# Which PSUM evictions the counting products wait for, in a convolution-attention and mixture-of-experts kernel

## The chip, the cores and the metric

The kernel runs on one core of one Trainium2 chip. The metric is the device time of one execution in microseconds; the time of the kernel before is the median of three runs.

## The reference, cut to what matters

Eight images of 256 channels by 32 x 32 positions pass two layers. Layer 0 projects each image to queries, keys and values (8 heads of 64), takes the softmax of the scores over the queries, and projects back. Layer 1 is an attention over the 1024 tokens of an image and then a mixture of 8 experts, of which each token uses its best two:

```python
logits = tokens.astype(jnp.float32) @ router_w.astype(jnp.float32).T
probs = jax.nn.softmax(logits, axis=-1)
rw, re = jax.lax.top_k(probs, TOP_K)
...
combine = jnp.zeros((N, E), tokens.dtype).at[jnp.arange(N)[:, None], re].set(rw)
...
for e in range(E):
    h = jax.nn.gelu(tokens @ w1[e] + b1[e], approximate=False)
    y = h @ w2[e] + b2[e]
    out = out + combine[:, e:e + 1] * y
```

Everything is float32.

## The kernel before, in words

The images go through the core one after the other (b = 0 to 7). For images 0 to 6 the tokens are sorted by expert and the experts run once over all seven images (`experts`); image 7 runs all experts over all its tokens (`dense`). To sort, the kernel needs for every token how many earlier tokens chose the same expert. It gets that from two small matrix products in `dispatch` (L820), here called the counting products: a strictly triangular matrix `before` (L832) and a matrix of ones (L833), each times `both`, the 128 x 64 table that marks the two experts of each token. Each writes 64 columns of PSUM. `d_cn` (L835) is VectorE's copy of the 128 columns into SBUF; the row addresses and the scatters to DRAM follow from it later.

`dispatch` is a generator. The routing of image b is advanced in steps by `share()` (L567) inside `layer0` of image b + 1, so the counting products run seven times, in layer 0 of images 1 to 7.

`layer0` (L441) walks 32 steps: four head pairs g, and for each eight blocks j of 128 keys. In a step, for two heads h, TensorE computes scores into a PSUM tile of two banks (`score`, L461, L468); VectorE takes the maximum of each bank (`first_max`, L483, and `second_max`, L492); ScalarE takes the exponential of both banks (`soften`, L509); VectorE divides (`divide`, L523, L525); and two steps later TensorE multiplies by the values (`gather_values`, L533, L545). The score tiles come from `ps_big`, a pool of three buffers of two banks each, in rotation.

At fixed steps (`PROJECT`, L454; step j = 3 for g = 0) the queries and keys of the next head pair are made by `project_pair` (L341). It takes one tile `pq` of that same pool and fills it twice, the queries first and then the keys. Each time, two products of 512 columns go to bank 0 and two to bank 1 (L350); each bank is then read out by ScalarE with the bias (`evict`, L315). So there are four evictions: queries bank 0, queries bank 1, keys bank 0, keys bank 1. They are called first to fourth below. The dependencies are kept by a tracker that sees one tile where there are two banks; where two accesses lie in different banks, the code takes the dependency away by hand (`declare_no_dep`, L359).

For g = 0 the counting products come directly after the eight products of `project_pair` (L621 to L623): `share(pq)` sends the tile to `dispatch`, and both counting products write columns 0 to 127 of it, which lie in bank 0. The next instructions of TensorE are held behind them by `issue_after(counted.ins)` (L579 to L588): the scores of the next step, `score(at, 0, 0)` and `score(at - 1, 1, 1)`, and then `gather_values(at - 2, 0)`. On VectorE, the copy to `d_cn` stands directly ahead of the second maximum of the interrupted step. On ScalarE the fourth eviction is followed by the exponential of that step.

Of the kernel before, what the change touches and what calls it, by code (L numbers as in the profile page):

```python
# [19 lines left out]
def kernel(  # L20
# [23 lines left out]
    nc = tc.nc  # L44
    P = 128
    B, C, S = x.shape
    E, D, FF = w1.shape
# [4 lines left out]
    NT = S // P  # L52
# [22 lines left out]
    def big(name):  # L75

        return ps_big.tile([P, 1024], F32, tag="big", name=name)
# [78 lines left out]
    ones = const.tile([P, P], F32, name="ones")  # L156
    nc.gpsimd.memset(ones, 1.0)

    before = const.tile([P, P], F32, name="before")
# [151 lines left out]
    def evict(dst, pq, g, t, scalar):  # L311

        scale = SCALE if t == 0 else 1.0
        if scalar:
            return nc.scalar.activation(  # L315
                dst, pq, AF.Identity, bias=b_qks[:, t, g : g + 1], scale=scale
            )
        return nc.vector.tensor_scalar(
            dst, pq, b_qk[:, t, g : g + 1], scale, ALU.add, ALU.mult
        )  # L320
# [20 lines left out]
    def project_pair(b, xT, g):  # L341


        pq = big(f"pqk_{b}_{g}")
        dsts, left = [], []
        for t in range(2):
            dst = two.tile([P, S], F32, tag=f"qk{t}", name=f"qk{t}_{b}_{g}")
            for n in range(NH2):
                for cc in range(NCC):
                    mm = nc.tensor.matmul(  # L350
                        pq[:, ts(n, 512)],
                        wqkv[:, cc, t, ts(g, P)],
                        xT[:, cc, ts(n, 512)],
                        start=(cc == 0),
                        stop=(cc == NCC - 1),
                    )
                    for at, ins in left:
                        if at != n:
                            tc.declare_no_dep(mm.ins, ins, reason="the other bank")  # L359
                left.append((n, evict(dst[:, ts(n, 512)], pq[:, ts(n, 512)], g, t, True).ins))  # L360
            dsts.append(dst)
        return dsts, pq, mm

    class Begin:

# [75 lines left out]
    def layer0(b, xT, begun, routing, xs):  # L441
# [132 lines left out]
        for at in range(last + LAG + 1):  # L574
# [38 lines left out]
            if at <= last and (g, j) in PROJECT:  # L613
                with tc.issue_after(firsts[at, 1].ins), tc.issue_after(array.ins):
                    share(firsts[at, 1])
                    pair, pq, mm = project_pair(b, xT, g + 1)
                qks.append(pair)
                if (g, j) == PROJECT[-1]:
                    with tc.issue_after(firsts[at, 1].ins):
                        t1 = residual(b, xs)  # L620
                if g == 0:  # L621
                    with tc.issue_after(mm.ins), tc.issue_after(firsts[at, 1].ins):
                        counted = share(pq)  # L623
                if b == B - 1 and (g, j) == PROJECT[-1]:
                    with tc.issue_after(firsts[at, 1].ins):
                        plan(groups[0])
            elif at <= last and (g, j) > PROJECT[1]:
                share(firsts[at, 1])
# [191 lines left out]
    def dispatch(b, n2, l, group):  # L820

        gate, hots = yield from gates(b, l)

        def tmp(tag):
            return small.tile([P, NT, E], F32, tag=tag, name=f"{tag}_{b}", bufs=1)


        both = tmp("d_both")
        nc.vector.tensor_add(both, hots[0], hots[1])
        pcn = yield  # L830
        flat = both.rearrange("p i e -> p (i e)")
        nc.tensor.matmul(pcn[:, : NT * E], before, flat, start=True, stop=True)  # L832
        counted = nc.tensor.matmul(pcn[:, NT * E : 2 * NT * E], ones, flat, start=True, stop=True)  # L833
        cn = small.tile([P, 2, NT, E], F32, tag="d_cn", name=f"d_cn_{b}", bufs=1)
        nc.vector.tensor_copy(cn.rearrange("p t i e -> p (t i e)"), pcn[:, : 2 * NT * E])  # L835
        yield counted
        per = small.tile([P, E, NT], F32, tag="d_per", name=f"d_per_{b}", bufs=1)
        nc.vector.tensor_copy(per, cn[:, 1].rearrange("p i e -> p e i"))
        upto = small.tile([P, E, NT], F32, tag="d_upto", name=f"d_upto_{b}", bufs=1)
        nc.vector.tensor_tensor_scan(  # L840
            upto.rearrange("p e i -> p (e i)"),
            later.rearrange("p e i -> p (e i)"),
            per.rearrange("p e i -> p (e i)"),
            0.0,
            ALU.mult,
            ALU.add,
        )
        rows = tmp("d_rows")
        nc.vector.tensor_sub(rows.rearrange("p i e -> p e i"), upto, per)
        nc.vector.tensor_add(rows, rows, cn[:, 0])  # L850
        counts = keep.tile([P, E], F32, tag="counts", name=f"counts_{b}")
        if group.counts is None:
            nc.vector.tensor_copy(counts, upto[:, :, NT - 1])
        else:
            nc.vector.tensor_add(
                rows, rows, group.counts.unsqueeze(1).to_broadcast([P, NT, E])
            )
            nc.vector.tensor_add(counts, group.counts, upto[:, :, NT - 1])
        group.counts = counts

        kept = []
        ats = []
        for k in range(2):
            hot = hots[k]
            sel = tmp("d_sel")
            nc.vector.tensor_mul(sel, hot, rows)
            row = keep.tile([P, NT], F32, tag=f"row{k}", name=f"row{k}_{b}")
            nc.vector.tensor_reduce(row, sel, AX.X, ALU.add)
            nc.vector.tensor_mul(sel, hot, e_iota.unsqueeze(1).to_broadcast([P, NT, E]))
            exp = keep.tile([P, NT], F32, tag=f"exp{k}", name=f"exp{k}_{b}")  # L870
            nc.vector.tensor_reduce(exp, sel, AX.X, ALU.add)
            to = small.tile([P, NT], F32, tag="d_to", name=f"d_to_{b}_{k}", bufs=2)
            nc.vector.scalar_tensor_tensor(to, exp, float(group.cap), row, ALU.mult, ALU.add)
            kept.append((row, exp))
            at = small.tile([P, NT], I32, tag=f"d_at{k}", name=f"d_at{k}_{b}", bufs=1)
            nc.vector.tensor_copy(at, to)
            ats.append(at)
        group.kept[b] = gate, kept

        for k in range(2):  # L880
            for i in range(NT):
                behind = yield
                view = group.views[2 * (NT * group.items.index(b) + i) + k]
                scatter = nc.gpsimd.indirect_dma_start(  # L884
                    out=view[:, :],
                    out_offset=bass.IndirectOffsetOnAxis(ap=ats[k][:, i : i + 1], axis=0),
                    in_=n2[:, i, :],
                    in_offset=None,
                )
                if behind is not None:  # L890
                    tc.add_manual_dep(scatter.ins, behind.ins.name, BEHIND)
# [420 lines left out]
    for b in range(B):  # L1312
        xT = next_x
        if b + 1 < B:
            next_x = load_x(b + 1)
        if b > 0:
            xs = load_squares(b)
        t1 = layer0(b, xT, begun, routing, xs)
        if b + 1 < B:
            begun = Begin(b + 1, next_x)  # L1320
            t2 = attend(b, t1, begun.at)
            n2, _, l = normed(b, t2, begun.at)
            nc.sync.dma_start(groups[0].sums[b], t2)
            routing = dispatch(b, n2, l, groups[0])
            continue
        experts(groups[0])
        others = Results(groups[0])
        others.begin()
        norm = None

        def fill(place):

            nonlocal norm
            others.tick(place)
            if place == "last products":
                norm = Norm(t1, one.tile([P, NT, D], F32, tag="xa", name=f"n2_{b}"), 1e-5, f"f{b}")
                return norm.blocks(0, NT - 1)

        t2 = attend(b, t1, fill, others.tick)
        dense(b, t2, norm, others.tick)  # L1340
        assert others.added == len(others.units) and not others.whole
# [42 lines left out]
```

## Time and profile before

| what | value |
| --- | --- |
| median of three runs (lowest, highest) | 2407.27 us (2404.34, 2408.37) |
| the profiled execution | 2406.31 us |
| its span in the profile | 2404.6 us, granted TensorE clock 0.994 |
| projections of a pair, L350 | 384 records, mean 599 ns |
| evictions, L315 | 124, mean 691 ns |
| counting products, L832 and L833 | 14 records each, mean 297 and 275 ns |
| copy to `d_cn`, L835 | 7, mean 291 ns |
| scores L468, gathered values L545 | 4096 records each, mean 594 and 592 ns |

The profile has one row per instruction, with a start and a duration, on separate tracks for TensorE's products (PE) and its weight loads (PEld), VectorE (DVE), ScalarE (ACT), GpSimd (POOL) and the DMA queue of SP. A float32 product appears as two records, each with its own weight load: 192 products on L350 make 384 records. A row of a timeline begins with start and duration, and may merge several records (x3 at its end); the duration then covers all of them. What stands in square brackets is the idle time of that track just before the row, and what ended it.

### The profile page before, as it was taken

How to read it: one execution, taken by the hardware profiler on the slowest of the kernel's cores; microseconds unless marked ns; L12 is line 12 of the kernel's file. 1: busy time of each engine (PE TensorE's matmuls, PEld its weight loads, DVE VectorE, ACT ScalarE, POOL GpSimd, SP SyncE). 2: the span in 40 equal slices, each digit the busy share in tenths (PEclk: the TensorE clock that was granted, in tenths of full speed). 3: DMA queues.
4: the chain of work that ended last, by engine and by line, in shares of the span. 5: the costliest groups of instructions: out<-in, count | busy, mean ns of one | idle time of the engine just before them, and what ended most of it. 6: DMA issues, size and time to landing. Idle time of an engine off the chain costs nothing.

```text
span 2404.6 us, 36813 instructions
## 1 busy us (share of the span) xinstructions
PE 2359.7 (98%) x13759; PEld 1316.5 (55%) x13759; DVE 1540.9 (64%) x3660; ACT 938.0 (39%) x1570; POOL 420.0 (17%) x391
## 2 busy tenths in 40 slices
PE   9999999999999999999999999999999999999898
PEld 3356534654466336633664356435653388887565
DVE  5775587457845785578647864687468753334776
ACT  3651366126611662156315641465136622221111
POOL 0000012000200020003000200020002234444563
PEclk9999999999999999999999999999999999999899
DMA  8993201010101010001000100100010256665454
GB/s 294 386 386 101 53 19 36 1 36 12 43 1 35 8 47 1 18 18 54 1 18 18 47 8 6 31 25 12 1 36 19 74 176 220 219 219 161 142 170 119
DMA packets 114778, 196.59 MB, mean 82 GB/s; under 512 B 15752, under 2 KB 58408, under 8 KB 112808
## 3 DMA queue, kind: packets, MB, share of 16 engines
q1 hardware_dynamic: 88504, 126.52, 15.8%
q0 software_dynamic: 25008, 67.20, 9.1%
q8 instruction: 109, 1.79, 0.3%
q10 hardware_dynamic: 1088, 0.52, 0.1%
q14 instruction: 69, 0.57, 0.1%
HBM read 108.88 MB, written 110.90 MB: 91 GB/s over the span
## 4 chain that ended last, share of the span: by engine, by line
PE 91%; DVE 5%; ACT 2%; DMA 1%; issue 1%; POOL 0%; SPq 0%; DVEq 0%; ACTq 0%; POOLq 0%
PE po L545 19%; PE psc L468 18%; PE py L695 9%; PE ps L670 7%; PE pqk L350 7%; PE pr L636 5%; PE ph L1021 4%; PE pv L387 4%; PE pe L1046 4%; PE pdh L1250 2%; PE px L655 2%; PE pdy L1274 2%; PE pa L689 2%; PE pqk L328 2%; PE px L1011 1%
## 5 line engine op out<-in xcount | busy, mean ns | idle before, releaser
L509 ACT ACTIVATE ex<-psc,nmax 128x1024 f32<-128x1024 f32 x512 | 570.5, 1115 | 312.6 <-DVE scrap L492 227.8
L468 PE MATMUL psc<-qk,qk 64*64 64x512 f32 x4096 | 578.4, 594 | 10.3 <-ACT ex L509 10.3
L545 PE MATMUL po<-ex,vs 64*64 64x512 f32 x4096 | 573.5, 592 | 1.3 <-DVE vs L525 0.3
L492 DVE TENSOR_SCALAR_CACHE_REDUCE scrap<-psc,nmax 128x512 f32<-128x512 f32 x512 | 384.4, 751 | 152.0 <-PE psc L468 126.2
L483 DVE TENSOR_REDUCE nmax<-psc 128x1 f32<-128x512 f32 x512 | 350.3, 684 | 9.3 <-PE psc L468 9.3
L468 PEld LDWEIGHTS psc<-qk,qk 64*64 64x64 f32 x4096 | 181.0, 132 | 285.8 <-ACT ex L509 138.0
L545 PEld LDWEIGHTS po<-ex,vs 64*64 64x64 f32 x4096 | 177.9, 132 | 273.5 <-issue 81.7
L695 PE MATMUL py<-n,aT 128*128 128x256 f32 x1024 | 238.0, 386 | 2.9 <-DVE aT L691 2.9
L670 PE MATMUL ps<-nT,xa 128*128 128x512 f32 x512 | 236.0, 592 | 0.0
L695 PEld LDWEIGHTS py<-n,aT 128*128 128x128 f32 x1024 | 191.7, 191 | 66.6 <-DVE aT L691 41.8
L884 POOL DMA_INDIRECT rows<-n,d_at x112 | 108.8, 972 | 662.6 <-DVE nmax L483 662.3
L681 ACT ACTIVATE ex<-ps,nmax 128x1024 f32<-128x1024 f32 x64 | 71.3, 1115 | 348.0 <-DVE nmax L678 333.5
L815 POOL TENSOR_TENSOR t<-t,n 128x2048 f32<-128x2048 f32 x8 | 36.3, 4534 | 924.0 <-DVE n L242 924.0
L350 PE MATMUL pqk<-xT,wqkv 128*128 128x512 f32 x384 | 171.2, 599 | 0.0
L701 DVE SCALAR_TENSOR_TENSOR t<-py,rs,t 128x256 f32<-128x256 f32 x64 | 30.9, 482 | 194.4 <-PE py L695 194.4
L670 PEld LDWEIGHTS ps<-nT,xa 128*128 128x128 f32 x512 | 93.5, 190 | 81.2 <-issue 75.1
L350 PEld LDWEIGHTS pqk<-xT,wqkv 128*128 128x128 f32 x384 | 71.0, 190 | 99.9 <-issue 77.8
L1130 POOL DMA_INDIRECT yk<-y,yat x112 | 110.6, 988 | 72.4 <-issue 26.8
L636 PEld LDWEIGHTS pr<-wo,res 128*128 128x128 f32 x512 | 120.7, 331 | 3.7 <-ACT res L563 3.7
L636 PE MATMUL pr<-wo,res 128*128 128x256 f32 x512 | 121.6, 398 | 0.3 <-ACT res L563 0.3
L387 PE MATMUL pv<-wqkv,xT 128*128 128x512 f32 x256 | 120.3, 599 | 1.4 <-DVE v L395 1.0
L315 ACT ACTIVATE qk<-pqk,b_qks 128x512 f32<-128x512 f32 x124 | 85.6, 691 | 88.9 <-PE pqk L350 79.8
(189 smaller groups left out, 2479.8 us busy)
## 6 DMA issues: line engine op xcount, KB each, us to landing
rows<-wb SPq DMA_DIRECT2D x7, 8192.0 KB, 51.7
y<-yb SPq DMA_DIRECT2D x63, 256.0 KB, 2.4
xs<-in_x_dram SPq DMA_DIRECT2D x64, 128.0 KB, 3.9
out_dram<-oT SPq DMA_DIRECT2D x60, 128.0 KB, 2.9
xT<-in_x_dram SPq DMA_DIRECT2D x7, 1024.0 KB, 5.0
sums<-t SPq DMA_DIRECT2D x7, 1024.0 KB, 3.9
o<-sums SPq DMA_DIRECT2D x7, 1024.0 KB
wpack<-in_L_ffn_w_dram SPq DMA_DIRECT2D x4, 1024.0 KB
```

What stands on the lines that cost most here:

```text
L350: mm = nc.tensor.matmul(pq[:, ts(n, 512)], wqkv[:, cc, t, ts(g, P)], xT[:, cc, ts(n, 512)], start=(cc == 0), stop=(cc == NCC - 1),)
L387: nc.tensor.matmul(pv, self.xT[:, cc, ts(i, P)], wqkv[:, cc, 2, :], start=(cc == 0), stop=(cc == NCC - 1),)
L468: mm = nc.tensor.matmul(pss[at, h][ts(c, DK), ts(n, 512)], k[r, j * P + c * DK : j * P + (c + 1) * DK], q[r, ts(n, 512)], start=True, stop ...
L483: firsts[at, h] = nc.vector.tensor_reduce(nmax, pss[at, h][:, ts(0, 512)], AX.X, ALU.max, negate=True)
L492: seconds[h] = nc.vector.tensor_scalar(scrap, pss[at, h][:, ts(1, 512)], -1.0, nmaxes[at, h], ALU.mult, ALU.min, accum_out=nmax,)
L509: nc.scalar.activation(ex, pss.pop((at, h)), AF.Exp, bias=nmaxes.pop((at, h)), scale=1.0, accum_out=sums[at][:, h : h + 1],)
L545: mm = nc.tensor.matmul(po[n][ts(h, DK), :], vss[at][keys, h, :], exps[at, h][keys, ts(n, 512)], start=(j == 0 and turn == 0), stop=(j == ...
L636: nc.tensor.matmul(pr[:, :C], own(res[:, g, :], i), wo[:, g, :], start=(g == 0), stop=(g == NPAIR - 1))
L670: nc.tensor.matmul(psc[:, ts(n, 512)], xa[:, ec, ts(i, P)], nT[:, ec, ts(n, 512)], start=(ec == 0), stop=(ec == NCC - 1),)
L695: nc.tensor.matmul(py[:, :D], aT[:, ts(m, P)], n1[:, m, :], start=(m == 0), stop=(m == NT - 1))
L884: scatter = nc.gpsimd.indirect_dma_start(out=view[:, :], out_offset=bass.IndirectOffsetOnAxis(ap=ats[k][:, i : i + 1], axis=0), in_=n2[:, ...
L1130: ins = nc.gpsimd.indirect_dma_start(out=self.slot(at)[:, k, :], out_offset=None, in_=self.group.y[:, :], in_offset=bass.IndirectOffsetOnAxis(
```

## The change

`project_pair` returns, with the tile, the list of those of its evictions that read bank 1. `dispatch` makes the same two counting products in a loop, and takes the dependency on those evictions away from each. The matrices, the columns and the order are as they were.

```diff
@@ project_pair @@
-        return dsts, pq, mm
+        return dsts, (pq, [ins for n, ins in left if n > 0]), mm
@@ dispatch @@
-        pcn = yield
+        pcn, others = yield
         flat = both.rearrange("p i e -> p (i e)")
-        nc.tensor.matmul(pcn[:, : NT * E], before, flat, start=True, stop=True)
-        counted = nc.tensor.matmul(pcn[:, NT * E : 2 * NT * E], ones, flat, start=True, stop=True)
+        for at, what in enumerate((before, ones)):
+            counted = nc.tensor.matmul(
+                pcn[:, ts(at, NT * E)], what, flat, start=True, stop=True
+            )
+            for ins in others:
+                tc.declare_no_dep(counted.ins, ins, reason="the other bank")
         cn = small.tile([P, 2, NT, E], F32, tag="d_cn", name=f"d_cn_{b}", bufs=1)
         nc.vector.tensor_copy(cn.rearrange("p t i e -> p (t i e)"), pcn[:, : 2 * NT * E])
         yield counted
```

In the built programs every engine has the same instructions in the same order before and after. Seven waits differ, one for each pair of counting products: the first of the pair waits for a count of ScalarE that is lower by one, so for the third eviction and no longer for the fourth. The copy to `d_cn` waits for the second counting product and for the fourth eviction in both programs.

## The prediction

> **What bounds the kernel now.** I read the page first: busy time by engine, then the chain that ended last.
>
> ```profile
> PE 2359.7 (98%) x13759; PEld 1316.5 (55%) x13759; DVE 1540.9 (64%) x3660; ACT 938.0 (39%) x1570; POOL 420.0 (17%) x391
> ...
> PE 91%; DVE 5%; ACT 2%; DMA 1%; issue 1%; POOL 0%; SPq 0%; DVEq 0%; ACTq 0%; POOLq 0%
> ```
>
> TensorE is the bound, so a hole in its stream that nothing else refills is lost time. The list of waits says whether the counting products make one (total us, times, longest):
>
> ```profile
> PEld pqk L832 <- ACT qk L315: 9.6, 6, 1.6
> ...
> PE pqk L832 <- ACT qk L315: 4.7, 6, 0.8
> ```
>
> Six of seven times TensorE waits for an eviction; the seventh, in image 1, is the same hole (0.83 us) under the name "issue". The timeline of the last one (start, duration, engine):
>
> ```profile
> 1792.86 0.69 ACT L315 ACTIVATE qk<-pqk,b_qks 128x512 f32<-128x512 f32 x1 [1.03 <-PE pqk L350]
> 1793.09 1.45 PE L350 MATMUL pqk<-xT,wqkv 128*128 128x512 f32 x3
> 1793.52 0.19 PEld L350 LDWEIGHTS pqk<-xT,wqkv 128*128 128x128 f32 x1 [0.24 <-issue]
> 1794.58 0.69 ACT L315 ACTIVATE qk<-pqk,b_qks 128x512 f32<-128x512 f32 x1 [1.03 <-PE pqk L350]
> 1795.31 0.30 PEld L832 LDWEIGHTS pqk<-d_both,before 128*128 128x128 f32 x2 [1.60 <-ACT qk L315]
> 1795.32 0.43 PE L832 MATMUL pqk<-d_both,before 128*128 128x64 f32 x2 [0.78 <-ACT qk L315]
> 1795.53 0.30 PEld L833 LDWEIGHTS pqk<-d_both,ones 128*128 128x128 f32 x2
> ...
> 1795.90 0.21 PEld L468 LDWEIGHTS psc<-qk,qk 64*64 64x64 f32 x8
> ...
> 1796.08 0.29 DVE L835 COPY d_cn<-pqk 128x128 f32<-128x128 f32 x1 [3.92 <-PE pqk L833]
> ...
> 1797.06 0.75 DVE L492 TENSOR_SCALAR_CACHE_REDUCE scrap<-psc,nmax 128x512 f32<-128x512 f32 x1 [0.69 <-PE psc L468]
> ```
>
> The first row is the third eviction, over at 1793.55; the fourth runs from 1794.58 to 1795.27, and the counting products start 0.04 us after it. I measure from the last weight load of the projection (1793.52, "t"): counting load t+1.79, scores t+2.38, copy t+2.56, maximum t+3.54. The other six agree within 0.03 us. In image 7, pair 1, the same projection stands without counting products:
>
> ```profile
> 1822.78 0.19 PEld L350 LDWEIGHTS pqk<-xT,wqkv 128*128 128x128 f32 x1 [0.24 <-issue]
> 1823.73 0.21 PEld L468 LDWEIGHTS psc<-qk,qk 64*64 64x64 f32 x8 [0.76 <-issue]
> ...
> 1824.64 1.04 PE L545 MATMUL po<-ex,vs 64*64 64x512 f32 x8
> ...
> 1824.89 0.75 DVE L492 TENSOR_SCALAR_CACHE_REDUCE scrap<-psc,nmax 128x512 f32<-128x512 f32 x1 [3.39 <-PE psc L468]
> ```
>
> Here the scores load at t+0.95, and the maximum starts at t+2.11, with no wait for the evictions. Seventeen such transitions (three in image 0, two in each other image) read 0.94 to 0.95.
>
> [...] the third eviction reads bank 0 while L350 writes bank 1, and takes 0.69 us like the fourth, beside which nothing is written. So I charge the new overlap nothing. [...] (loads of L350 are 0.43 us apart, beside running products)[...]. [...] so I count from starts, and not from the bracketed 0.78.
>
> **The change, part by part.** Nothing is added or moved: same instructions, same order on all queues, SP's and POOL's included. What goes is one count in the wait of seven instructions.
>
> When can the first counting product go? Its three conditions: the third eviction, over at t+0.03 and, with 0.04 to 0.07 us to be seen, at t+0.10; the table `both`, done at t-1.35 in six cases and t-3.68 in the first; the queue, whose next slot is one spacing after t, t+0.43. The queue is last. The load of `before` is 128 x 128 like L350's, so I let it be pulled ahead: t+0.43. The product behind it starts when the last L350 record has streamed, t+0.86, and the second load with it. The loads then follow at their present pace (four from 1795.31 to about 1795.64, 0.11 apart; scores 0.26 after the fourth): t+0.86, t+0.97, t+1.08, scores t+1.34. Against t+2.38 to t+2.41 that is 1.05 us. A second way: the plain transition, 0.95, plus four records of 0.11, is t+1.39, a gain of 1.00. I take 1.05; 7 x 1.05 = 7.35 us.
>
> Bounds of one gain: if the counting load isn't pulled ahead, it starts where the scores do in the plain transition, t+0.95, and the scores at t+0.95+0.59 = t+1.54: 0.85. The bracketed gap gives 0.78. If all follows at the next slot, 1.79 - 0.43 = 1.36, the largest gain possible[...]. Seven times: 5.5 to 9.5 us.
>
> What is late next? VectorE: the copy still waits for the fourth eviction, which doesn't move (t+1.06 to t+1.75). It starts at about t+1.81 and ends at t+2.10. The second maximum queued behind it needs its score, t+3.54 - 1.05 = t+2.49: 0.39 us of slack. If that cover were gone, the copy's 0.29 us would be exposed. ScalarE: the exponential now starts 0.86 us after the maximum does; it moves to about t+3.3, and ScalarE is free from t+1.75. PSUM: the score tile that takes over `pq`'s buffer starts over a microsecond after the scores restart, past the copy's new end. TensorE then runs steps of 3.43 us without a hole, as after every transition now.
>
> The sum: profiled execution 2406.31 (span 2404.6 and 1.7 around it) less 7.35 is 2399.0. It lay 1.0 under the median of 2407.27, so I forecast 2407.27 - 7.35 = 2399.9.
>
> **The rivals.**
> *Load not pulled ahead.* The plain transition speaks for it (loads wait there), the equal tile size against it. 7 x 0.85 = 6.0: 2401.3.
> *The copy stays the pace.* The copy has two waits; if VectorE starts it only where it does now, t+2.56, the maximum comes at t+2.86 and not at t+2.49. The gain is 3.54 - 2.86 = 0.68; seven make 4.8: 2402.5. For it: the copy does wait for the fourth eviction. Against: that ends 0.8 us before t+2.56.
> *Given back.* The layer norm behind layer 0, or the DMA-fed expert stage, could be tied to something that doesn't move: 2407. Against: all transfers of a stage are issued behind its own instructions, and the chain is 91% TensorE.
> *Slower: the score ring falls out of step.* VectorE has only 0.32 us idle in a step of 3.43 (two gaps, 0.19 and 0.13). If TensorE restarts earlier than VectorE by more than it regains, score tiles come free late and TensorE waits for the exponential in each of the four steps left of the pair. The waits list has weight loads waiting for that 216 times, 138.0 us, so 0.64 each: 7 x 4 x 0.64 = 17.9 us lost, 7.35 won: 2417.8. It decides from the point where the copy ends more than 0.32 us after t+2.49. Against: the plain transitions restart at t+0.95, earlier than any forecast here, and keep 3.43 us.
>
> That the edit does nothing is excluded: the seven waits differ in the built program.
>
> **How the numbers follow.** Chances: forecast 0.63, load not pulled ahead 0.15, copy 0.12, given back 0.07, slower 0.03. A measurement of this kernel tells about 0.2% (4.8 us, below 2402.5) from no change. Faster: 0.63 + 0.15 + half of the copy's 0.12 = 0.84; within: 0.06 + 0.07 = 0.13; slower 0.03. The bounds give 2407.27 - 9.5 = 2397.8 and - 5.5 = 2401.8, and 2402.5 with the copy; a median of three runs that spread over 4 us may be off by about one: 2396.8 to 2403.2. Left out are given back and slower, 0.10, and about as much for the spread.
>
> **What would show it.** Right: the wait of L832's product for the eviction is gone; its load starts at t+0.43, the scores' at t+1.34, the copy at t+1.8, the maximum at t+2.5, and seven such gains make up the span's loss. The load at t+0.95 shows the first rival; a maximum later than its score, the second; weight loads of L468 waiting longer for L509, the last. I am wrong if the scores come over 1.0 us earlier and the span doesn't.

## The result and the profile after

The changed kernel takes 2397.39 us (median of six runs, 2396.64 to 2400.2) against 2407.69 us for the kernel before in the same measurement. The ratio is 0.996, with a 95% interval of 0.9947 to 0.9973. It is faster, by 0.4%. The forecast was 2399.9; the measured time lies 2.5 us below it, inside the stated range and near its lower end. A second measurement of the same kernel, on another occasion, is among the experiments (e8_again): 2398.23 against 2406.58.

The page after the change, busy time and chain:

```profile
PE 2353.9 (98%) x13759; PEld 1313.9 (55%) x13759; DVE 1541.2 (64%) x3660; ACT 938.0 (39%) x1570; POOL 420.4 (18%) x391
...
PE 90%; DVE 5%; DMA 2%; ACT 1%; issue 1%; POOL 0%; SPq 0%; DVEq 0%; ACTq 0%; POOLq 0%
```

The totals hardly move, and would not have shown where the gain comes from. The list of waits does (total us, times, longest):

```profile
DVE d_cn L839 <- ACT qk L315: 24.2, 7, 5.4
...
PEld pqk L833 <- issue: 3.4, 14, 0.2
```

The rows in which the counting products wait for an eviction are gone. The first two weight loads of each pair follow the stream, with 0.2 us of idle track ahead of them. The wait for the eviction has moved to VectorE's copy. The last of the seven places in the timeline (start, duration, engine; line numbers behind L832 are four higher than before, and both counting products are now on L833):

```profile
1787.24 0.19 PEld L350 LDWEIGHTS pqk<-xT,wqkv 128*128 128x128 f32 x1 [0.24 <-issue]
1787.67 0.19 PEld L833 LDWEIGHTS pqk<-d_both,before 128*128 128x128 f32 x1 [0.24 <-issue]
...
1788.10 0.19 PEld L833 LDWEIGHTS pqk<-d_both,before 128*128 128x128 f32 x1 [0.24 <-issue]
1788.21 0.30 PEld L833 LDWEIGHTS pqk<-d_both,ones 128*128 128x128 f32 x2
...
1788.30 0.69 ACT L315 ACTIVATE qk<-pqk,b_qks 128x512 f32<-128x512 f32 x1 [1.03 <-PE pqk L350]
1788.58 0.21 PEld L468 LDWEIGHTS psc<-qk,qk 64*64 64x64 f32 x8
...
1789.02 0.29 DVE L839 COPY d_cn<-pqk 128x128 f32<-128x128 f32 x1 [3.13 <-ACT qk L315]
...
1789.74 0.75 DVE L492 TENSOR_SCALAR_CACHE_REDUCE scrap<-psc,nmax 128x512 f32<-128x512 f32 x1 [0.43 <-PE psc L468]
```

With t = 1787.24, the last weight load of the projection, the row of the fourth eviction (1788.30) now stands behind the counting loads and beside their products. The scores load at t+1.34 in place of t+2.38.

To take the whole effect of the seven places out of a trace, I subtract the start of the last weight load of L350 ahead of the first counting products (298.81 before, 298.79 after) from that of the last one of image 7 (1857.47 and 1850.15). This stretch holds all seven places and no stage behind layer 0 of image 7. It was 1558.66 us before and is 1551.36 after: 7.30 us shorter, 1.04 a place. Nothing else in it differs: with the two traces laid on each other weight load by weight load, the lead of the changed kernel grows by 1.04 to 1.06 us within 5 us of each place, and until the next place it moves by 0.02 us at most. The rest, from that last load to the end of the span, was 547.1 before and is 545.2 after.

### The profile page after: what moved, and what is told of

Its sections match the earlier page's. It is cut to its first block, busy times and chain, and to the rows that moved or that the text cites. A ratio compares the mean times of both kernels' runs of the same rounds, so it can differ in the third digit from the quotient of the medians.

```text
span 2395.3 us, 36813 instructions
## 1 busy us (share of the span) xinstructions
PE 2353.9 (98%) x13759; PEld 1313.9 (55%) x13759; DVE 1541.2 (64%) x3660; ACT 938.0 (39%) x1570; POOL 420.4 (18%) x391
## 4 chain that ended last, share of the span: by engine, by line
PE 90%; DVE 5%; DMA 2%; ACT 1%; issue 1%; POOL 0%; SPq 0%; DVEq 0%; ACTq 0%; POOLq 0%
PE po L545 19%; PE psc L468 18%; PE py L695 8%; PE ps L670 7%; PE pqk L350 7%; PE pr L636 5%; PE pv L387 4%; PE ph L1025 4%; PE pe L1050 4%; PE pdh L1254 2%; PE px L655 2%; PE pdy L1278 2%; PE pa L689 2%; PE pqk L328 2%; PE px L1015 1%
## 5 line engine op out<-in xcount | busy, mean ns | idle before, releaser
L509 ACT ACTIVATE ex<-psc,nmax 128x1024 f32<-128x1024 f32 x512 | 570.5, 1115 | 304.1 <-DVE scrap L492 220.4
L468 PE MATMUL psc<-qk,qk 64*64 64x512 f32 x4096 | 577.4, 593 | 10.3 <-ACT ex L509 10.3
L545 PE MATMUL po<-ex,vs 64*64 64x512 f32 x4096 | 573.2, 592 | 1.3 <-DVE vs L525 0.3
L468 PEld LDWEIGHTS psc<-qk,qk 64*64 64x64 f32 x4096 | 180.7, 132 | 285.9 <-ACT ex L509 138.3
L545 PEld LDWEIGHTS po<-ex,vs 64*64 64x64 f32 x4096 | 177.6, 132 | 273.0 <-issue 81.2
L695 PE MATMUL py<-n,aT 128*128 128x256 f32 x1024 | 236.3, 384 | 2.9 <-DVE aT L691 2.9
L695 PEld LDWEIGHTS py<-n,aT 128*128 128x128 f32 x1024 | 190.5, 190 | 66.1 <-DVE aT L691 41.8
L350 PE MATMUL pqk<-xT,wqkv 128*128 128x512 f32 x384 | 171.2, 599 | 0.0
L350 PEld LDWEIGHTS pqk<-xT,wqkv 128*128 128x128 f32 x384 | 71.0, 190 | 99.9 <-issue 77.8
```

The lines of the kernel that those rows point to most:

```text
L350: mm = nc.tensor.matmul(pq[:, ts(n, 512)], wqkv[:, cc, t, ts(g, P)], xT[:, cc, ts(n, 512)], start=(cc == 0), stop=(cc == NCC - 1),)
L468: mm = nc.tensor.matmul(pss[at, h][ts(c, DK), ts(n, 512)], k[r, j * P + c * DK : j * P + (c + 1) * DK], q[r, ts(n, 512)], start=True, stop ...
L509: nc.scalar.activation(ex, pss.pop((at, h)), AF.Exp, bias=nmaxes.pop((at, h)), scale=1.0, accum_out=sums[at][:, h : h + 1],)
L545: mm = nc.tensor.matmul(po[n][ts(h, DK), :], vss[at][keys, h, :], exps[at, h][keys, ts(n, 512)], start=(j == 0 and turn == 0), stop=(j == ...
L695: nc.tensor.matmul(py[:, :D], aT[:, ts(m, P)], n1[:, m, :], start=(m == 0), stop=(m == NT - 1))
```

## The experiments

All times after t are read as above. "The stretch" and "the rest" are those just defined, taken from each kernel's profile:

| kernel | scores load | stretch | rest | median (runs) | before beside it |
| --- | --- | --- | --- | --- | --- |
| before | t+2.38 to 2.41 | 1558.66 | 547.1 | | |
| after | t+1.34 | 1551.36 | 545.2 | 2397.39 (6) | 2407.69 |
| e1_bank1 | t+2.38 to 2.41 | 1558.71 | 548.4 | 2406.31 (12) | 2406.41 |
| e2_three | three 1.34, four 2.38 | 1555.55 | 549.9 | 2403.18 (12) | 2406.41 |
| e3_copy_free | t+1.34 | 1551.33 | 545.7 | 2399.74 (7) | 2406.41 |
| e4_four_copies | t+1.34 | 1554.22 | 548.8 | 2402.81 (12) | 2406.41 |
| e5_before_twice | t+3.10 to 3.12 | 1563.55 | 552.8 | 2411.56 (9) | 2406.58 |
| e6_after_twice | t+1.34 | 1551.15 | 549.4 | 2398.97 (6) | 2406.58 |
| e7_bf16 | t+1.01 | 1548.98 | 547.3 | 2396.83 (5) | 2406.58 |
| e8_again | t+1.34 | 1551.29 | 548.8 | 2398.23 (7) | 2406.58 |

The stretch repeats within 0.1 us for the same behaviour (after, e3, e8). The rest scatters over 7.6 us whatever the kernel, so the stretch is the sharper gauge of this change. The first four experiments ran on one chip, e5 to e8 on another, each with the kernel before beside them.

**e1_bank1: the same number of dependencies taken away, but the wrong ones.** The counting products go to columns 512 to 639 of the tile, and lose their dependency on the evictions of bank 0.

```diff
-        return dsts, (pq, [ins for n, ins in left if n > 0]), mm
+        return dsts, (pq, [ins for n, ins in left if n == 0]), mm
...
-                pcn[:, ts(at, NT * E)], what, flat, start=True, stop=True
+                pcn[:, 512 + at * NT * E : 512 + (at + 1) * NT * E], what, flat, start=True, stop=True
...
-        nc.vector.tensor_copy(cn.rearrange("p t i e -> p (t i e)"), pcn[:, : 2 * NT * E])
+        nc.vector.tensor_copy(cn.rearrange("p t i e -> p (t i e)"), pcn[:, 512 : 512 + 2 * NT * E])
```

> The counting products write bank 1 of the same tile and wait only for evictions that read bank 1; as many dependencies are taken away as in the change. Times after t, the start of the last weight load of the projection. Theory (what counts is which eviction ends the wait): the products wait for the fourth eviction again, counting load at t+1.8, scores at t+2.4, layer 0 of image 7 reaches its last projection load at 1857.5 us as before, time within 0.2% of before (2407.7). Rival (it is the smaller number of dependencies, or the loop form of the code, that gains): counting load at t+0.43 and a time as after, 2397.

Measured: ratio to before 0.9998 (0.999 to 1.0007), stretch 1558.71. The last place in its timeline:

```profile
1793.39 0.19 PEld L350 LDWEIGHTS pqk<-xT,wqkv 128*128 128x128 f32 x1 [0.24 <-issue]
1794.45 0.69 ACT L315 ACTIVATE qk<-pqk,b_qks 128x512 f32<-128x512 f32 x1 [1.03 <-PE pqk L350]
1795.19 0.30 PEld L833 LDWEIGHTS pqk<-d_both,before 128*128 128x128 f32 x2 [1.61 <-ACT qk L315]
```

The load waits for the end of the fourth eviction, as in the kernel before. So neither the loop form nor the smaller number of dependencies gains anything; what counts is which eviction is the last one waited for.

**e2_three: the change at three places of seven.**

```diff
         pcn, others = yield
+        others = others if b < 3 else []
```

> The change for the counting products of images 0 to 2 only, three places of seven. Theory (each place gives 1.05 us, independently): three transitions with scores at t+1.34 and four at t+2.39; the last projection load of image 7 at 1857.5 - 3.2 = 1854.3 us, time before less 3.2 us, 2404.5, give or take what the tail behind layer 0 does by itself. Rival (the whole measured gain of 10.3 us belongs to the places, 1.47 each): the last projection load at 1853.1, time before less 4.4, 2403.3. Rival (steps behind a place slow down again): last load near 1857.

Measured: three transitions at t+1.34, four at t+2.38 to 2.39; the stretch is 3.11 us shorter than before, 1.04 a place. The median is 3.2 us lower (ratio 0.9988, 0.998 to 0.9997). The gain adds up place by place, and no step behind a place gives any of it back. The median alone would not exclude 4.4; the stretch does, as far as layer 0 goes.

**e3_copy_free: the copy doesn't wait for bank 1 either.**

```diff
-        nc.vector.tensor_copy(cn.rearrange("p t i e -> p (t i e)"), pcn[:, : 2 * NT * E])
+        copied = nc.vector.tensor_copy(
+            cn.rearrange("p t i e -> p (t i e)"), pcn[:, : 2 * NT * E]
+        )
+        for ins in others:
+            tc.declare_no_dep(copied.ins, ins, reason="the other bank")
```

> The change, and the copy to d_cn no longer waits for the evictions of bank 1 either. Theory (the copy had slack): it starts at about t+1.4 in place of t+1.78, the second maximum behind it stays at t+2.50 because it waits for its score, the scores stay at t+1.34, and the time is that of after (2397 to 2398). Rival (the copy paces VectorE, which paces the restart): the maximum comes earlier by up to 0.35 us and the time falls by up to 7 x 0.35 = 2.5 us against after.

Measured: the copy starts at t+1.52 in place of t+1.78, the second maximum still at t+2.50, the stretch is 1551.33 as after. Median 2399.74, ratio to before 0.9972 (0.9961 to 0.9984); that is above the 2397 to 2398 expected, by a difference that the stretch does not show. The copy had slack, and its wait for the fourth eviction costs nothing.

**e4_four_copies: VectorE's slack taken away.**

```diff
-        nc.vector.tensor_copy(cn.rearrange("p t i e -> p (t i e)"), pcn[:, : 2 * NT * E])
+        for _ in range(4):
+            nc.vector.tensor_copy(cn.rearrange("p t i e -> p (t i e)"), pcn[:, : 2 * NT * E])
```

> The change, and the copy to d_cn is made four times in a row, so that VectorE's cover is gone: copies from t+1.78 to about t+3.1, the second maximum at about t+3.1 in place of t+2.50, so 0.6 us late. Theory (VectorE's idle 0.32 us in each step of 3.43 us takes part of it up, the rest is a stall of TensorE once per image): between 0 and 7 x 0.6 = 4.3 us slower than after, 2397.4 to 2401.7. Rival (the score ring falls out of step when VectorE restarts too late): TensorE waits in all four steps left, over 10 us slower than after, above 2407.

Measured: the four copies take 1.27 us and the maximum comes at t+2.96, 0.46 late (I had expected 0.6). The stretch is 2.86 us longer than after. Laid load by load on the trace of the changed kernel, 0.29 us is lost within 6 us of each of the seven places, 2.0 in all; the other 0.8 is lost at three spots far from them (0.16 at a later projection of image 1, 0.35 in a layer norm, 0.3 shortly before the last place but one), and why there is open. The loss at the last place (t = 1789.52):

```profile
1791.30 1.27 DVE L840 COPY d_cn<-pqk 128x128 f32<-128x128 f32 x4 [3.14 <-ACT qk L315]
...
1792.49 0.74 DVE L492 TENSOR_SCALAR_CACHE_REDUCE scrap<-psc,nmax 128x512 f32<-128x512 f32 x1
...
1793.33 1.11 ACT L509 ACTIVATE ex<-psc,nmax 128x1024 f32<-128x1024 f32 x1 [2.06 <-DVE scrap L492]
...
1794.59 0.21 PEld L468 LDWEIGHTS psc<-qk,qk 64*64 64x64 f32 x8 [0.82 <-ACT ex L509]
```

The late maximum makes the exponential late; the exponential releases a score tile; and the scores of two steps on load at t+5.07. After the change that load comes at t+4.61, after a wait of 0.49 which the products in flight cover: those of L545 run from t+3.97 to t+5.01, and those of the load start at t+4.82. In the same list of waits, loads of L468 wait for L509 217 times and 140.8 us, against 216 and 138.3 after. So the stall comes once per place, and is not repeated in each step left: the score ring doesn't fall out of step. The median, 2402.81, stays below before (ratio 0.9985, 0.9976 to 0.9994). It is 3.1 us above e3 on the same chip, and 1.1 above the range expected.

**e5_before_twice and e6_after_twice: the fourth eviction lengthened.** Both the kernel before and the changed kernel make the fourth eviction of the first pair twice; the second writes the same values again.

```diff
                 left.append((n, evict(dst[:, ts(n, 512)], pq[:, ts(n, 512)], g, t, True).ins))
+                if g == 1 and t == 1 and n == 1 and b > 0:
+                    left.append((n, evict(dst[:, ts(n, 512)], pq[:, ts(n, 512)], g, t, True).ins))
```

> The kernel before, with the fourth eviction (keys, bank 1) of the first pair made twice in images 1 to 7, 0.69 us more of ScalarE at each place. Theory (the fourth eviction ends the wait): counting load at about t+2.5 in place of t+1.8, scores at about t+3.1, 7 x 0.72 = 5 us slower than before, 2411.4; last projection load of image 7 at 1862.5. Rival (something else, that ends at the same time, releases the products): no change, 2406.4 and 1857.5.

> The changed kernel with the same doubled fourth eviction. Theory: products and scores do not feel it, t+0.43 and t+1.34; but the copy to d_cn still waits for the last eviction and goes from t+1.78 to about t+2.5, the second maximum behind it from t+2.50 to about t+2.8, 0.3 us late. The run with four copies lost 0.37 us a place with a maximum 0.46 late, so 0.1 to 0.3 here: 0.7 to 2 us slower than the changed kernel, last projection load at 1850.9 to 1852.1. So 9 to 12 us faster than the kernel before with the doubled eviction. Rival (the copy has no part in the restart): last load at 1850.1, no loss at all.

The last place of e5_before_twice; the two evictions are merged in one row (x2):

```profile
1797.67 0.19 PEld L350 LDWEIGHTS pqk<-xT,wqkv 128*128 128x128 f32 x1 [0.24 <-issue]
1798.72 1.41 ACT L315 ACTIVATE qk<-pqk,b_qks 128x512 f32<-128x512 f32 x2 [1.03 <-PE pqk L350]
1800.18 0.30 PEld L834 LDWEIGHTS pqk<-d_both,before 128*128 128x128 f32 x2 [2.33 <-ACT qk L315]
```

The wait has grown from 1.60 to 2.33 us, and the stretch by 4.89 us, 0.70 a place. The median is 5.0 us above before (ratio 1.0019, 1.001 to 1.0029). The same edit on the changed kernel:

```profile
1786.79 0.19 PEld L350 LDWEIGHTS pqk<-xT,wqkv 128*128 128x128 f32 x1 [0.24 <-issue]
1787.22 0.19 PEld L835 LDWEIGHTS pqk<-d_both,before 128*128 128x128 f32 x1 [0.24 <-issue]
...
1787.85 1.41 ACT L315 ACTIVATE qk<-pqk,b_qks 128x512 f32<-128x512 f32 x2 [1.03 <-PE pqk L350]
...
1789.29 0.29 DVE L841 COPY d_cn<-pqk 128x128 f32<-128x128 f32 x1 [3.86 <-PE psc L470]
...
1789.50 0.74 DVE L494 TENSOR_SCALAR_CACHE_REDUCE scrap<-psc,nmax 128x512 f32<-128x512 f32 x1
...
1790.28 1.11 ACT L511 ACTIVATE ex<-psc,nmax 128x1024 f32<-128x1024 f32 x1 [1.02 <-DVE scrap L494]
...
1791.54 0.24 PEld L470 LDWEIGHTS psc<-qk,qk 64*64 64x64 f32 x8 [0.62 <-ACT ex L511]
...
1791.62 1.04 PE L470 MATMUL psc<-qk,qk 64*64 64x512 f32 x8
```

The products go ahead undisturbed. The copy comes at t+2.50, 0.03 us after the second of the two evictions ends (what its row names is a product of scores, which by the profile ended last). The maximum comes at t+2.71, 0.21 late, and the stretch is 1551.15: nothing is lost. I had expected 0.7 to 2 us, so this was a miss.

What takes the lateness up can be read in three traces. VectorE's idle time brings its next maximum back in time, to t+4.18 in both kernels. The exponential is only 0.14 us late (t+3.49 in place of t+3.35), and the load of scores that it releases comes at t+4.75 in place of t+4.61. After the change the products of that load start at t+4.82, so the load has 0.21 us in hand; here they start at t+4.83. In e4 the load comes at t+5.07 and its products with it, 0.25 late, which is most of the 0.29 lost at a place. The expected 0.1 to 0.3 a place came from scaling e4's loss down, as if there were no such reserve.

**e7_bf16: the remainder of the place made smaller.** The tables hold only zeros and ones, and the sums go up to 128, so the products can be made in bfloat16.

```diff
+    BF16 = mybir.dt.bfloat16
+    halves = const.tile([P, 2, P], BF16, name="halves")
+    nc.gpsimd.tensor_copy(halves[:, 0, :], before)
+    nc.gpsimd.tensor_copy(halves[:, 1, :], ones)
...
-        both = tmp("d_both")
+        both = small.tile([P, NT, E], BF16, tag="d_half", name=f"d_half_{b}", bufs=1)
...
-        for at, what in enumerate((before, ones)):
+        for at, what in enumerate((halves[:, 0, :], halves[:, 1, :])):
```

> The changed kernel with the counting products in bfloat16 (the tables hold only 0 and 1), to make the rest of the place smaller. One record in place of two for each product. Expected from the spacings of the changed kernel: loads at t+0.43 and t+0.86, scores at about t+1.12 in place of t+1.34, 0.22 us a place, 1.5 us in all: last projection load at 1848.6, time 1.5 us below the changed kernel, which the total can hardly show. Rival (a change of number format in TensorE's stream costs a stop of its own[...]): scores not before t+1.34, no gain or a loss of up to 3.5 us.

```profile
1785.09 0.19 PEld L355 LDWEIGHTS pqk<-xT,wqkv 128*128 128x128 f32 x1 [0.24 <-issue]
1785.52 0.10 PEld L838 LDWEIGHTS <-halves 128*128 128x128 bf16 x1 [0.24 <-issue]
...
1785.95 0.10 PEld L838 LDWEIGHTS <-halves 128*128 128x128 bf16 x1 [0.33 <-issue]
1786.09 0.21 PEld L473 LDWEIGHTS psc<-qk,qk 64*64 64x64 f32 x8
```

Two loads in place of four, each 0.10 us, and the scores at t+1.00 to 1.01: 0.33 us a place, more than the 0.22 expected. The rival is out; the loss of up to 3.5 us that it names was my estimate, seven times about 0.5 us, the 0.95 of a plain transition less the 0.43 between loads of L350. The stretch is 1548.98, 2.3 us shorter than in e8_again. The median is 2396.83 against 2398.23 of e8_again on the same chip, ratio to before 0.9965 (0.9951 to 0.9978). It is the fastest version tried, but the intervals of the two overlap; only the traces separate them. A transition without counting products has its scores at t+0.95, so the counting products now add 0.06 us to it.

**e8_again: the changed kernel once more.** No edit.

> The changed kernel once more, unaltered, to size the measured gain. Seven places give 7.35 us; the first measurement gave 10.3. Theory (what goes beyond 7.35 is scatter of the stages behind layer 0, whose length from the last projection load to the end was 545.2 to 549.9 us in six profiles, whatever the kernel): last projection load at 1850.1 again, a gain of 6 to 9 us this time. Rival (the change shortens the stages behind layer 0 as well): again about 10 us, and 545 us behind the last projection load.

Measured: 2398.23 against 2406.58, 8.4 us less (ratio 0.9968, 0.9956 to 0.9979). The stretch is 1551.29, as in the first profile of this kernel; the rest is 548.8 this time instead of 545.2.

## Why the prediction was right, point by point

**TensorE is the bound and the hole is the fourth eviction's.** Shown. Lengthen that eviction by 0.72 us, and the kernel before slows by 0.70 us a place (e5); move the products to the bank it reads, and the gain disappears (e1, stretch 1558.71 against 1558.66).

**The next limit is the queue's slot, t+0.43.** Right at all seven places: loads at t+0.43, 0.86, 0.97 and 1.08, scores at t+1.34, each as forecast. The counting load stands 0.43 us behind the last projection load, at the start of that load's product, which the profile shows from t+0.43 to t+1.02; so the rival in which it waits until t+0.95 is out. That it would keep the spacing of the loads of L350 was my estimate, and so was the bound of 1.36 us a place, which no run tested. Both loads are 128 x 128; into the 64 x 64 scores of a plain transition the step is 0.95 us.

**The fourth eviction is not slowed by the counting products beside it.** It takes 0.69 us as before (t+1.06 to t+1.75), while the counting products write bank 0 beside it (t+0.86 to t+1.41). So nothing had to be charged for this overlap.

**VectorE is late by nothing.** The copy came at t+1.78 (forecast t+1.81), the maximum at t+2.50 (t+2.49), the exponential at t+3.35 (t+3.3). The slack is real: freeing the copy changes nothing (e3), delaying the maximum by 0.21 us changes nothing (e6), by 0.46 it costs 0.29 at each place (e4). So the rival of the copy is out for this kernel, and its price is known at these two points should the copy grow.

**The slower rival.** Its trigger was forced: in e4 the copies end at t+3.05, 0.56 us later than the forecast t+2.49 of the maximum and past the stated 0.32; in e6 the copy ends at t+2.79, 0.30 later, and nothing is lost. TensorE then stalled for the exponential as the rival said, but once per place and not in four steps. The term of 17.9 us was too large by a factor of six: 2.86 measured, of which 2.0 at the places. The rival also names only VectorE's idle time as the reserve; what took up the 0.21 us in e6 lies in part on TensorE's own track.

**Given back.** Not inside the stretch: the lead of the changed kernel stays what it is from one place to the next (e2 shows the same with three places).

**The sum.** 7.35 us forecast, 7.30 measured in the stretch. The total fell by 10.3 us in the first measurement and by 8.4 in the second; in e3 and e6, which lose nothing at the places either, by 6.7 and 7.6. All four intervals of the ratio contain 7.35/2407. In the eight later measurements the median differs from that of the kernel before by what the stretch does, to within 1.0 us either way and by nothing on average; the first one, with six runs of each kernel, is 3.0 off. The 3 us by which the first total fell further than forecast are not repeated, so they are taken as scatter and not as a part of the effect that the forecast missed.

What scatters is the rest, whose length goes from 545.2 to 552.8 us over ten profiles without following the edits. A large part lies in one piece of it. From the weight load (L695) that starts at 2251 us in the changed kernel to the one (L1278 there) that starts at 2300, the same instructions take 48.8 to 48.9 us in three profiles with a granted clock of 0.93 there (after, e3, e4), 50.4 to 50.6 in three at 0.90 (e2, e6, e7), and 50.6 to 53.4 in four at 0.81 to 0.87 (before, e1, e5, e8). The two profiles of the changed kernel, which are the same program, are among the first and the last: 3.2 of the 3.6 us between their rests arise in this piece. Likewise the profiles before and after differ by 2.0 us in the rest, all of it there. What lengthens the other pieces, by up to 3.6 us, was not separated, and a help of the change to the rest that is well under a microsecond cannot be excluded; nothing requires it.

## What to carry to other kernels

When an engine waits for several readers of one tile, ask which reader ends last and whether it touches what the waiter writes: one unneeded dependency on the last reader cost a full 1.04 us here, against 0.78 us of visible gap. The gap counts from the end that the profile gives the last projection product, t+1.02, and in the changed kernel the next product starts 0.16 us ahead of that, at t+0.86; and one of the four loads, which stood 0.11 us apart before, now runs beside the projection product. 0.78, 0.16 and 0.10 make up the 1.04. A transition of the same kind elsewhere in the trace, without the wait, gives the size of the gain before any run. Where the total scatters by several microseconds in stages that the change doesn't touch, time a stretch of the trace that holds the change and nothing else.

## What the runs showed of the hardware that was not expected

- A 128 x 64 product in bfloat16 between float32 ones cost no stop of its own: its weight load took 0.10 us against 0.19 in float32, and the 64 x 64 float32 scores loaded 0.14 us after the last bfloat16 load, where they load 0.26 us after the last float32 one.
- The granted clock reads 1.00 over the first 1850 us in the kernel before and in both profiles of the changed one, and the stretch, nearly all of it inside these 1850 us, repeats within 0.1 us. In windows of 50 us behind that it is 0.93 at 1850 to 1900 us in all ten profiles, and 0.83 to 0.94 at 2250 to 2300 us, where the same instructions take between 48.8 and 53.4 us.
